# Side tasks queued ahead of the mask and exp of their step, in a two-layer graph kernel

## The chip, the core and the metric

The kernel runs on one core of a Trainium2 chip. The metric is the device time of one launch in microseconds (us). Before the change it was 3613.7 us, the median of three runs (3613.04 to 3614.69); the profiled execution took 3614.43 us, with a span of 3612.6 us from first to last instruction and a granted TensorE clock of 0.994.

## The reference

The first layer is a graph convolution over a 2048-node graph with two batch norms; the second is attention over the same graph, with 4 heads of 64, where only pairs with a nonzero entry in the adjacency take part. Each layer ends with a residual sum and a layer norm.

```python
# layer 0: A_hat @ features, two linear layers with batch norm
agg = jnp.einsum('nm,bmd->bnd', A_hat, features)
...
out = _batchnorm(out, g2, be2)
x = _layernorm(x + _L0_gnn_ref(...), axis=-1)
# layer 1: masked attention
qkv = h @ W
scores = jnp.einsum('bhid,bhjd->bhij', q, k) / np.sqrt(HEAD_DIM) + mask
attn = jax.nn.softmax(scores, axis=-1)
out = jnp.einsum('bhij,bhjd->bhid', attn, v)
x = _layernorm(x + _L1_gnn_ref(x, L1_gnn_W, adj), axis=-1)
```

x is 8 x 2048 x 256 in float32, so there are 8 batches, and everything is computed in float32.

## The kernel before

The change touches the second layer alone, which begins at about 1276 us and takes the other two thirds of the span. The attention is cut into 64 units: 8 batches, 2 pairs of heads, 4 chunks of 512 query columns. A unit has 16 steps, one for each tile of 128 keys. The loop variable `g` counts the steps over all units; `u` is the unit and `j` the step in it.

One step does this for its tile:

- `scores` (L842, TensorE): q times k, in 64x64 pieces for two heads, into a PSUM tile `st`, of which there are two.
- `mask_scores` (L854, VectorE): adds the mask to `st` and writes the SBUF tile `prob`, of which there are 13.
- `exps` (L860, ScalarE): exp of `prob` in place.
- `weigh` (L872, TensorE): `prob` times v, summed over the 16 steps in the PSUM tile `out_ps`.
- `add_up` (L882 to L893, GpSimd): sums `prob` tiles for the softmax's denominator, partly with adding transfers.

`scores`, `mask_scores` and `exps` run three steps ahead of `weigh` (`LEAD = 3`): in step `g` of the loop stand the scores, mask and exp of tile `g + 3` and the weighing of tile `g`.

Beside this there are side tasks: the projections of q, k and v of coming units, the normalization of the next batch's input, and the end of the unit before (its sums, the division by them, the residual, the layer norm, the output). Each has a due time, `at_step(u, j, f, ...)`: the whole part of `j` names the step, and the tasks of a step run in the order of `j`. A due time that is a whole number, such as 6, and one with a fraction, such as 6.1, were treated alike before. The tasks that the text speaks of:

- `finish_sums` (due 6): matmuls with ones (L909) sum `acc` over its partitions into a PSUM tile `pm`; ScalarE copies it out as `sm` (L917).
- `project` (before: due 0.1, 6.1, 10.1, for q, k, v): matmuls into `pm` (L777 for q and k, L791 for v); q and v are copied out by ScalarE (L782, L798), k by VectorE (L786).
- `norm` (half 0 due 6.2, half 1 due 0 of the next unit): four transposes into `pm` (L711), then on VectorE the residual sum (L719) and statistics (L660, L662). It runs in 28 units.
- `finish_turn_sums` (due 10): two transposes of `sm` (L923), a copy and a reciprocal on VectorE (L925, L930); `finish_turn` (10.2) transposes the unit's output (L936), and `finish` (10.3 and, before, 11) divides and adds on VectorE (L944).
- `emit` (due 4 and 5) and `apply` (due 7 and 8): each half is two normalizing activations on ScalarE (L672). `bn` (due 3.5 and 4.7): one each on ScalarE (L696).
- `turn` (due 13 and 13.2): four transposes for each half (L740) and a copy on ScalarE (L746). `emit_stats` (due 12.5 and 14): statistics on VectorE. `root` (due 3 or 15.5): four small operations on GpSimd.

All the `pm` tiles come from one PSUM pool with two buffers, taken in turn: a task that asks for one waits until the use before last has been read out. The engines TensorE, VectorE, ScalarE and GpSimd run their instructions in the order in which this loop emits them (`manual_schedule`), so the order of the Python calls is the order of each queue. Waits between engines are semaphores that the framework puts in.

Of the kernel before, what the change touches and what calls it, by code (L numbers as in the profile page):

```python
# [26 lines left out]
def tile_gcn_then_masked_attention(  # L27
# [169 lines left out]
    with tc.tile_pool(name="bt7", bufs=1, side="right") as bp7, tc.tile_pool(  # L197
# [20 lines left out]
        for n, t in enumerate(order):  # L218
# [7 lines left out]
            j, m = divmod(t, HT)  # L226
            k, q = divmod(m, TPC)
            here = slice(q * P, (q + 1) * P)
            for g in range(NT // 4):
# [4 lines left out]
                i, m0 = divmod(4 * g, HT)  # L234
# [574 lines left out]
    def attention():  # L809


        with tc.tile_pool(
# [8 lines left out]
            inp = Layer1Input(ip, ps_m, NCH + 4)  # L821
# [11 lines left out]
            def scores(g):  # L833
                u, j = divmod(g, NT)
                b, hp, c = units[u]
                qt, kt, _ = inp.qkv[b, hp]
                cols = slice(c * CH, (c + 1) * CH)
                st = ps_s.tile([P, 2, CH], F32, name="st")
                for h in range(2):
                    hs = slice(h * HD, (h + 1) * HD)  # L840
                    for r in range(2):
                        nc.tensor.matmul(  # L842
                            st[r * HD : (r + 1) * HD, h, :],
                            kt[hs, j * P + r * HD : j * P + (r + 1) * HD],
                            qt[hs, cols],
                            start=True, stop=True,
                        )
                return st

            def mask_scores(g, st):  # L850
                j, cols = g % NT, units[g // NT][2] * CH
                cols = slice(cols, cols + CH)
                p = probs[g] = ap_.tile([P, 2, CH], F32, name="prob", bufs=13)
                nc.vector.scalar_tensor_tensor(  # L854
                    p, mask[:, j, cols][:, None, :].to_broadcast([P, 2, CH]), MASKED, st,
                    op0=ALU.mult, op1=ALU.add,
                )

            def exps(g):
                nc.scalar.activation(probs[g], probs[g], AF.Exp)  # L860
# [34 lines left out]
            def finish_out(u):  # L895
                ots[u] = ap_.tile([P, CH], F32, name="ot")
                nc.scalar.copy(ots[u], outs[u][:, 0, :])
                nc.vector.tensor_add(ots[u], outs.pop(u)[:, 1, :], ots[u])  # L898
# [69 lines left out]
            side = {}  # L968

            def at_step(u, j, f, *args):  # L970
                tasks = side.setdefault((u, int(j)), [])
                tasks.append((j, f, args))
                tasks.sort(key=lambda task: task[0])

            per_b = HP * NCH
            for u in range(NU):
                b, hp, c = units[u]
                at_step(u + 1, 6, finish_sums, u)
                at_step(u + 1, 10, finish_turn_sums, u)
                at_step(u + 1, 10.2, finish_turn, u)  # L980
                at_step(u + 1, 10.3, finish, u, 0)
                at_step(u + 1, 11, finish, u, 1)
                if u == NU - 2:
                    for half in range(2):
                        at_step(u + 1, 11.3 + half, inp.emit_stats, b, c, half)
                        at_step(u + 1, 14 + half, inp.emit, b, c, half)
                    at_step(u + 1, 12.5, inp.root, b, c)
                elif u == NU - 1:
                    for half in range(2):
                        at_step(u + 1, 10.4 + half, inp.emit_stats, b, c, half)  # L990
                        at_step(u + 1, 10.5 + half, inp.root_half, b, c, half)
                        at_step(u + 1, 12 + half, inp.emit_half, b, c, half)
                    at_step(u + 1, 14, count_sums)
                elif hp == HP - 1:
                    for half in range(2):
                        at_step(u + 1, 12.5 + 1.5 * half, inp.emit_stats, b, c, half)
                        at_step(u + 2, 4 + half, inp.emit, b, c, half)
                    at_step(u + 1, 15.5, inp.root, b, c)

            PROJECT = (0.1, 6.1, 10.1)

            def project_at(u, b, hp, c):
                for w in range(3):
                    at_step(u, PROJECT[w], inp.project, b, hp, c, w)

            for b in range(B):
                u0 = b * per_b
                if b:  # L1010
                    project_at(u0, b, 0, NCH - 1)
                for c in range(NCH):
                    project_at(u0 + 1 + c, b, 1, c)
                    if b + 1 == B:
                        continue
                    u = u0 + 3 + c
                    at_step(u, 1, inp.load_y, b + 1, c)
                    at_step(u, 1, inp.load_x, b + 1, c)
                    for o in range(NO):
                        at_step(u, 3.5 + 1.2 * o, inp.bn, b + 1, c, o)  # L1020
                    at_step(u, 6.2, inp.norm, b + 1, c, 0)
                    at_step(u + 1, 0, inp.norm, b + 1, c, 1)
                    at_step(u + 1, 3, inp.root, b + 1, c)
                    for half in range(2):
                        at_step(u + 1, 7 + half, inp.apply, b + 1, c, half)
                        at_step(u + 1, 13 + 0.2 * half, inp.turn, b + 1, c, half)
                    if c < NCH - 1:
                        project_at(u + 2, b + 1, 0, c)
# [3 lines left out]
                for half in range(2):  # L1032
                    at_step(0, j, inp.turn, 0, c, half)
            for half in range(2):
                at_step(0, 1, inp.apply, 0, 3, half)
            for j, c, w in (
                (1.1, 1, 2), (2.1, 2, 1), (5.1, 2, 2), (6.1, 3, 1), (8.1, 1, 0), (10.1, 3, 2)
            ):
# [4 lines left out]
            with tc.manual_schedule(engines=IN_ORDER):  # L1043
                for c in range(NCH):
                    inp.yt[0, c] = y0[c]
                    inp.x1[0, c] = ip.tile([P, TPC, D], F32, name="x1", bufs=NCH + 4)
                    for o in range(NO):
                        inp.bn(0, c, o)

                def ready(c):  # L1050
                    pm = ps_s.tile([P, TPC, D], F32, name="st")
                    for half in range(2):
                        pmh = pm[:, half * IT : (half + 1) * IT, :]
                        inp.turn_y(0, c, half, pmh)
                        inp.add_y(0, c, half, pmh, x0[c])
                    inp.root(0, c)

                def halves(f, c):
                    for half in range(2):
                        f(0, c, half)  # L1060

                for c in range(NCH - 1):
                    ready(c)
                halves(inp.apply, 0)
                halves(inp.turn, 0)
                halves(inp.apply, 1)
                inp.project(0, 0, 0, 1, k_on_act=True)
                inp.project(0, 0, 0, 0)
                ready(NCH - 1)
                right.close()  # L1070
                ap_ = inp.y_pool = late.enter_context(
                    tc.tile_pool(name="attn", bufs=2, side="right", reuse_waits="tile")
                )
                inp.project(0, 0, 0, 2)
                halves(inp.turn, 1)
                for g in range(LEAD):
                    mask_scores(g, scores(g))
                    exps(g)
                    if g == 1:
                        inp.project(0, 0, 1, 1)  # L1080
                        halves(inp.apply, 2)
                for g in range(NU * NT):
                    u, j = divmod(g, NT)
                    ahead = g + LEAD < NU * NT
                    if ahead:
                        st = scores(g + LEAD)
                    if j == NT - 1:
                        weigh(g)
                        finish_out(u)
                    if ahead:  # L1090
                        mask_scores(g + LEAD, st)
                        exps(g + LEAD)
                    for _, f, args in side.get((u, j), ()):
                        f(*args)
                    if j < NT - 1:
                        weigh(g)
                    add_up(g)
                for u in (NU, NU + 1):
                    for j in range(NT):
                        for _, f, args in side.get((u, j), ()):  # L1100
                            f(*args)

    def attention_with_maxima():

        with tc.tile_pool(name="full", bufs=2) as ap_, tc.tile_pool(
# [9 lines left out]
            for b in range(B):  # L1115
# [55 lines left out]
                for c in range(NCH):  # L1171
# [3 lines left out]
                    for half in range(2):  # L1175
                        inp.emit(b, c, half)

    attention()


# [46 lines left out]
```

## Time and profile before

| Engine | busy us | share of the span |
| --- | --- | --- |
| TensorE (matmul) | 3553.4 | 98% |
| GpSimd | 2265.8 | 63% |
| VectorE | 1994.5 | 55% |
| ScalarE | 1635.0 | 45% |

| Durations, second layer | mean us of one | number |
| --- | --- | --- |
| mask L854 (VectorE) | 1.218 | 1024 |
| exp L860 (ScalarE) | 1.056 | 1024 |
| sum of prob tiles L893 (GpSimd) | 2.60 | 319 |
| copy of sm L917 (ScalarE) | 0.353 | 64 |
| normalizing activation L672 (ScalarE) | 0.586 | 256 |

The first table reads: TensorE is almost never without a matmul, and every other engine is idle for over a third of the span. The second says how long a side task holds an engine in comparison with the mask or exp of a step; in the timeline a step of scores and weighing without side tasks takes 1.72 us (scores start at 1550.57, 1552.29, 1554.01 us and so on).

### The profile page before, as it was taken

The numbers are of one execution on the slowest core, as the hardware profiler recorded it, in microseconds if no ns is written. First come the engines' busy times: TensorE is split into PE (matmuls) and PEld (weight loads), VectorE is DVE, ScalarE is ACT, GpSimd is POOL, SyncE is SP. The second block draws the span as 40 slices with busy tenths as digits, with TensorE's granted clock in tenths as the row PEclk, the third lists the DMA queues.
The fourth block names the chain that finished last, engine by engine and source line by source line (L and its number), as shares of the span: only waits on it lengthen the run. The fifth ranks groups of instructions, "written<-read, shape, count | busy, mean of one in ns | idle before, by whom it ended". The sixth has DMA issues, their size and how long they took to land.

```text
span 3612.6 us, 55141 instructions
## 1 busy us (share of the span) xinstructions
PE 3553.4 (98%) x22503; PEld 1469.7 (41%) x22503; DVE 1994.5 (55%) x2929; ACT 1635.0 (45%) x2036; POOL 2265.8 (63%) x1530
## 2 busy tenths in 40 slices
PE   8999999999999899999999999999999999999997
PEld 5444444444444443433333333333343334343332
DVE  6212141221146656676766776676666677667666
ACT  5101100110135455655565565565566566556555
POOL 3543263434247647776777677777777777777777
PEclk9999999999999999999999999999999999999999
DMA  9122232231247345666565666556566556555655
GB/s 340 65 72 88 81 134 82 76 96 32 82 187 267 143 91 103 127 126 123 112 141 119 119 131 132 108 123 141 112 123 133 117 112 148 112 117 113 122 109 115
DMA packets 197142, 440.14 MB, mean 122 GB/s; under 512 B 14080, under 2 KB 121104, under 8 KB 186384
## 3 DMA queue, kind: packets, MB, share of 16 engines
q0 software_dynamic: 64656, 239.37, 35.0%
q1 hardware_dynamic: 132048, 196.11, 15.8%
q8 instruction: 178, 2.92, 0.3%
q10 hardware_dynamic: 176, 1.06, 0.1%
q14 instruction: 84, 0.69, 0.1%
HBM read 126.62 MB, written 75.51 MB: 56 GB/s over the span
## 4 chain that ended last, share of the span: by engine, by line
PE 95%; ACT 2%; DVE 2%; POOL 1%; DMA 0%; issue 0%; DVEq 0%; POOLq 0%; ACTq 0%; SPq 0%
PE out_ps L872 25%; PE st L842 24%; PE pa L333 21%; PE ph L366 5%; PE pm L777 5%; PE pa L543 5%; PE pm L791 3%; DVE prob L854 1%; PE pm L711 1%; ACT prob L860 1%; PE pm L740 1%; PE pm L936 1%; PE pm L923 1%; PE ps L233 1%; PE pm L909 1%; PE ph L588 1%
## 5 line engine op out<-in xcount | busy, mean ns | idle before, releaser
L854 DVE SCALAR_TENSOR_TENSOR prob<-mask,st 128x1024 f32<-128x1024 uint8 x1024 | 1242.0, 1218 | 486.1 <-PE st L842 412.2
L860 ACT ACTIVATE prob<-prob 128x1024 f32<-128x1024 f32 x1024 | 1081.0, 1056 | 930.0 <-DVE prob L854 838.5
L872 PE MATMUL out_ps<-prob,v 64*64 64x512 f32 x8192 | 1074.2, 595 | 2.7 <-DVE ot L898 1.7
L842 PE MATMUL st<-qt,kt 64*64 64x512 f32 x8192 | 1062.8, 589 | 0.1
L893 POOL TENSOR_TENSOR acc<-acc,prob 128x1024 f32<-128x1024 f32 x319 | 829.7, 2601 | 8.0 <-DMA prob<-prob 2.6
L333 PE MATMUL pa<-t,x 128*128 128x512 f32 x1792 | 773.4, 594 | 2.7 <-ACT x L309 2.7
L882 POOL DMA_DIRECT2D prob<-prob x447 | 403.7, 928 | 582.5 <-PE out_ps L872 503.3
L842 PEld LDWEIGHTS st<-qt,kt 64*64 64x64 f32 x8192 | 312.6, 133 | 566.7 <-issue 538.0
L333 PEld LDWEIGHTS pa<-t,x 128*128 128x128 f32 x1792 | 341.4, 191 | 432.7 <-issue 428.7
L872 PEld LDWEIGHTS out_ps<-prob,v 64*64 64x64 f32 x8192 | 290.7, 133 | 541.6 <-issue 445.7
L414 POOL TENSOR_TENSOR ag<-ag,dbc 128x512 f32<-128x512 f32 x16 | 20.2, 1261 | 486.3 <-DVE ag L413 454.8
L884 POOL TENSOR_TENSOR acc<-acc,prob 128x1024 f32<-128x1024 f32 x126 | 298.1, 2366 | 7.5
L370 ACT ACTIVATE h<-ph,b1s 128x512 f32<-128x512 f32 x112 | 76.9, 687 | 404.4 <-PE ph L366 404.4
L777 PE MATMUL pm<-x1t,wq 128*128 128x512 f32 x512 | 253.1, 617 | 0.7 <-ACT x1t L746 0.7
L394 ACT COPY ag<-pa 128x512 f32<-128x512 f32 x16 | 9.4, 585 | 422.9 <-PE pa L333 409.8
L366 PE MATMUL ph<-ag,w1s 128*128 128x512 f32 x448 | 193.4, 592 | 0.0
L891 POOL TENSOR_TENSOR acc<-prob 128x1024 f32<-128x1024 f32 x64 | 171.2, 2675 | 1.7 <-DMA prob<-prob 1.7
L944 DVE SCALAR_TENSOR_TENSOR x<-pm,ri,x 128x64 f32<-128x64 f32 x512 | 109.6, 277 | 62.4 <-PE pm L936 61.7
L672 ACT ACTIVATE x<-x,ln_nm,ln_rs 128x256 f32<-128x256 f32 x256 | 137.6, 586 | 10.5 <-POOL ln_nm L668 10.5
L777 PEld LDWEIGHTS pm<-x1t,wq 128*128 128x128 f32 x512 | 87.8, 191 | 119.8 <-issue 113.0
L371 DVE BATCH_NORM_STATS2 st<-h 128x6 f32<-128x512 f32 x112 | 76.9, 692 | 99.1 <-ACT h L370 99.1
L366 PEld LDWEIGHTS ph<-ag,w1s 128*128 128x128 f32 x448 | 85.1, 190 | 107.1 <-issue 106.9
(139 smaller groups left out, 2609.0 us busy)
## 6 DMA issues: line engine op xcount, KB each, us to landing
prob<-prob POOLq DMA_DIRECT2D x447, 512.0 KB, 4.9
x<-in_x_dram SPq DMA_DIRECT2D x92, 512.0 KB, 5.4
h_d<-h SPq DMA_DIRECT2D x28, 1024.0 KB, 3.9
t<-h_d SPq DMA_DIRECT2D x28, 1024.0 KB, 8.2
a<-in_adj_dram SPq DMA_DIRECT2D x16, 1024.0 KB, 5.0
y_d<-ag SPq DMA_DIRECT2D x32, 512.0 KB, 2.6
out_dram<-x SPq DMA_DIRECT2D x31, 512.0 KB, 4.9
yt<-y_d SPq DMA_DIRECT2D x28, 512.0 KB, 3.3
```

The lines of the kernel that those rows point to most:

```text
L333: nc.tensor.matmul(pa, s.t[:, m, :], t[:, m, :], start=(m == 0), stop=(m == HT - 1))
L366: nc.tensor.matmul(ph, w1s[:, d, f * P : (f + 1) * P], ag[:, d, :], start=(d == 0), stop=(d == ND - 1),)
L543: nc.tensor.matmul(py, w[:, f, :], t[:, f, :], start=(f == 0), stop=(f == 1))
L777: nc.tensor.matmul(pm, wq[:, d, wcols], xt[:, d, cols], start=(d == 0), stop=(d == ND - 1))
L842: nc.tensor.matmul(st[r * HD : (r + 1) * HD, h, :], kt[hs, j * P + r * HD : j * P + (r + 1) * HD], qt[hs, cols], start=True, stop=True,)
L854: nc.vector.scalar_tensor_tensor(p, mask[:, j, cols][:, None, :].to_broadcast([P, 2, CH]), MASKED, st, op0=ALU.mult, op1=ALU.add,)
L860: nc.scalar.activation(probs[g], probs[g], AF.Exp)
L872: nc.tensor.matmul(outs[u][hs, r, :], inp.qkv[b, hp][2][rs, j, hs], probs[g][rs, h, :], start=(j == 0), stop=(j == NT - 1),)
L882: nc.gpsimd.dma_start(probs[g - 1], probs[g], accum_op=ALU.add)
L884: nc.gpsimd.tensor_add(accs[u], accs[u], probs[g])
L891: nc.gpsimd.tensor_add(accs[v], probs[g - 7], probs[g - 5])
L893: nc.gpsimd.tensor_add(accs[v], accs[v], probs[g - 5])
```

## The change

Side tasks whose due time is exactly a whole step are now called before the mask and exp of that step, and those with a fraction after them, as before. The call of `scores` stays ahead of all of them and that of `weigh` behind. Four due times that were whole, or had to stay behind a task that was moved, get another fraction, so that these tasks keep their places: `finish` half 1, `norm` half 1, the projection of q, and the `apply` of the first unit.

The purpose is that work which others wait for, such as the copy of `sm` out of PSUM, doesn't stand in its engine's queue behind a mask or exp that nobody needs for three steps.

```diff
-                at_step(u + 1, 11, finish, u, 1)
+                at_step(u + 1, 11.1, finish, u, 1)
...
-            PROJECT = (0.1, 6.1, 10.1)
+            PROJECT = (0.2, 6.1, 10.1)
...
-                    at_step(u + 1, 0, inp.norm, b + 1, c, 1)
+                    at_step(u + 1, 0.1, inp.norm, b + 1, c, 1)
...
-                at_step(0, 1, inp.apply, 0, 3, half)
+                at_step(0, 1.05, inp.apply, 0, 3, half)
...
                     if j == NT - 1:
                         weigh(g)
                         finish_out(u)
+
+                    tasks = side.get((u, j), ())
+                    for i, f, args in tasks:
+                        if i == j:
+                            f(*args)
                     if ahead:
                         mask_scores(g + LEAD, st)
                         exps(g + LEAD)
-                    for _, f, args in side.get((u, j), ()):
-                        f(*args)
+                    for i, f, args in tasks:
+                        if i > j:
+                            f(*args)
                     if j < NT - 1:
                         weigh(g)
                     add_up(g)
```

## Prediction

> **What bounds the kernel now.** I read the page's first part, then its chain of waits, then the list of who TensorE waited for, then the timeline around the longest entry.
>
> ```profile
> PE 3553.4 (98%) x22503; PEld 1469.7 (41%) x22503; DVE 1994.5 (55%) x2929; ACT 1635.0 (45%) x2036; POOL 2265.8 (63%) x1530
> PE 95%; ACT 2%; DVE 2%; POOL 1%; DMA 0%; issue 0%; DVEq 0%; POOLq 0%; ACTq 0%; SPq 0%
> ```
>
> TensorE sets the time: 95% of the chain that ended last is its own work. What a reordering of other engines can win is at most its idle time, 3612.6 - 3553.4 = 59 us, or 1.6%. The waits of TensorE (us in total, times, longest) say where that idle time is:
>
> ```profile
> PE pm L711 <- ACT sm L917: 15.7, 28, 1.4
> PE st L711 <- ACT ag L696: 6.1, 2, 5.9
> PE pc L243 <- DMA a<-in_adj_dram: 5.8, 1, 5.8
> PE pm L909 <- POOL acc L893: 3.6, 1, 3.6
> PE out_ps L872 <- ACT prob L860: 1.0, 1, 1.0
> ```
>
> The first line is the only one that recurs through the attention: 28 times the transposes of `norm` wait for the copy of `sm`. The second and third lie before the attention, the last two after the last scores. At step 6 `finish_sums` takes one `pm` buffer, `project` the other, and `norm` wants the first again, which is free once ScalarE has copied `sm`. The timeline shows what that copy stands behind (start us, duration us, engine, line):
>
> ```profile
> 1410.11 1.06 ACT L860 ACTIVATE prob<-prob 128x1024 f32<-128x1024 f32 x1
> 1410.39 0.64 PE L909 MATMUL pm<-acc,ones 128*32 128x256 f32 x8
> 1410.96 1.98 PE L777 MATMUL pm<-x1t,wq 128*128 128x512 f32 x4
> 1411.85 1.06 ACT L860 ACTIVATE prob<-prob 128x1024 f32<-128x1024 f32 x1 [0.68 <-DVE prob L854]
> 1412.81 0.35 ACT L917 COPY sm<-pm 128x256 f32<-128x256 f32 x1
> 1413.22 0.66 PE L711 MATMUL pm<-ident,yt 128*128 128x128 f32 x4 [0.28 <-ACT sm L917]
> 1413.81 1.09 PE L872 MATMUL out_ps<-prob,v 64*64 64x512 f32 x8
> ```
>
> The sums are ready at 1410.39 + 0.64 = 1411.03, and ScalarE is idle from 1411.17. But the step's exp is ahead in its queue, waiting for the mask until 1411.85; so the copy ends only at 1413.16. The second form of the wait is longer:
>
> ```profile
> 2103.47 1.98 PE L777 MATMUL pm<-x1t,wq 128*128 128x512 f32 x4
> 2103.58 1.04 ACT L860 ACTIVATE prob<-prob 128x1024 f32<-128x1024 f32 x1
> 2104.53 1.08 ACT L672 ACTIVATE x<-x,ln_nm,ln_rs 128x256 f32<-128x256 f32 x2
> 2105.51 1.04 ACT L860 ACTIVATE prob<-prob 128x1024 f32<-128x1024 f32 x1
> 2106.45 0.35 ACT L917 COPY sm<-pm 128x256 f32<-128x256 f32 x1
> 2106.86 0.66 PE L711 MATMUL pm<-ident,yt 128*128 128x128 f32 x4 [1.41 <-ACT sm L917]
> ```
>
> Here the unit also has `emit` and `bn` in steps 3 to 5, ScalarE runs without a pause since 2099.19, and the exp is late itself. One unit per batch boundary is of this kind: two pairs of heads end while the next batch is normalized. With n long and 28 - n short waits, 1.41 n + 0.28 (28 - n) = 15.7 gives n = 7, as seven batch boundaries should.
>
> **What the Trainium skill says.** "TensorE: Matmul & The Clock Gate", section "Architectural detail: the array is 16× 32×32, not 1× 128×128", states that ScalarE and VectorE queues are strictly first in, first out, while TensorE may pull weight loads ahead. The trace agrees: ScalarE idles 0.68 us before the exp with a ready copy behind it. "Perfetto Trace Analysis", section "Tensor Engine Instruction (MATMUL, LD_WEIGHTS)", states that the end of a matmul in the profile is a model. The trace agrees: L777's bar of 1.98 us is overlapped by the next matmul, 1.92 us after its start where nothing is waited for. I therefore price waits by start to start, not by the idle figures.
>
> **The change part by part.** TensorE, GpSimd and the DMA queue keep the order of their instructions; only ScalarE and VectorE are reordered. No operation is added or removed.
>
> 1. *Copy of `sm` (63 of 64 units).* The three windows from the scores of step 6 to the next weighing, which the timeline gave, are
>
> ```profile
> 1409.42:1413.81 4.39, 4.11 (x29) 1.41 (x21) 2.53 (x3) 3.07 (x5) 0.00 (x0) 1.00 0.89 166
> 1559.16:1562.61 3.45, 3.45 (x25) 0.99 (x17) 1.83 (x2) 3.45 (x7) 1.55 (x2) 1.00 0.73 134
> 2101.93:2107.44 5.51, 4.11 (x28) 1.41 (x20) 2.52 (x3) 4.87 (x9) 1.57 (x2) 1.00 0.83 155
> ```
>
> (first number: length). The second has no `norm`. Four transposes with no wait take 0.53 us from start to start (L936 at 1571.70, L872 at 1572.23). So the short wait really costs 4.39 - 3.45 - 0.53 = 0.41 us, the long one 5.51 - 3.98 = 1.53. After the change the copy of the short case starts at 1411.17, when the exp before it ends, and is out by 1411.6; `norm` may start at 1410.96 + 1.92 = 1412.88. The wait goes: 21 x 0.41 = 8.6 us. In the long case ScalarE is saturated, and its queue up to the copy is shorter by one exp only, which takes 2106.45 - 2105.51 = 0.94 us from start to start. The transposes move from 2106.86 to 2105.92, where 2103.47 + 1.92 = 2105.39 would be free: 0.53 us of wait stay. Gain 7 x 0.94 = 6.6 us. **Sum 15.2 us.** In the other units nobody waits for the copy, and nothing is won.
>
> 2. *What the copy delays.* The exp behind it, by 0.35 us at most, and the semaphore wait on L909, which is done 0.14 us before ScalarE is free. The exp's tile is weighed three steps, over 5 us, later. Cost 0.
>
> 3. *`finish_turn_sums` (63 times).* VectorE now holds the mask of step 10 until the transposes L923 are done: 1420.84 + 0.44 = 1421.28, then 0.17 + 0.20 for copy and reciprocal, so the mask starts near 1421.7 instead of 1420.97 and ends near 1422.9. Behind it: `finish` half 0, which waits for TensorE until 1423.54 anyway; the exp and the copy of v, 0.7 us later; and the scores of step 12, which need this `st` buffer only at 1426.05. `finish_turn` gets its `pm` sooner than before. Cost 0, with 3 us of slack.
>
> 4. *`emit` and `apply` (58 units' worth, two halves of 1.07 us on ScalarE) ahead of an exp.* Their inputs come from `root` steps earlier (done 2101.39, used from 2111.75), so they don't wait; an exp comes up to 1.07 us later. In the saturated unit the last late exp ends near 2106.9 and is weighed after 2111. Cost 0, hidden behind scores and weighing.
>
> 5. *`turn` half 0 and `emit_stats` half 1.* The copy L746 (0.58) fits into ScalarE's pause before the exp at 2085.73, the statistics (0.75 + 0.30) into VectorE's 1.15 us before the mask at 2086.84. Cost 0. `root` and the loads stand on queues without mask or exp.
>
> 3613.7 - 15.2 = **3598.5 us**, 0.42% less.
>
> **The rivals.**
>
> - *The long waits go too.* If the applied activations start in earlier pauses, ScalarE is not saturated at the copy: 21 x 0.41 + 7 x 1.53 = 19.3 us, 3594.4. Against it: no pause is left from 2099.19 on.
> - *Only the short waits go.* If `emit`'s move hands the 0.94 us back in the seven long units: 3613.7 - 8.6 = 3605.1. For it: ScalarE is full there. Against: the work ahead of the copy gets less whatever the order.
> - *The wait moves on.* The time saved at `norm` is lost at the weighing behind it, to GpSimd (busy for 1591 of 2160 us in the attention) or to an exp: 3612, no difference. Against: weighings show no wait on either in the attention.
> - *Slower.* If the mask of step 10, 0.7 us later in 63 units, reached the path, 63 x 0.7 = 44 us would be lost against 15 won: 3643 at worst. The scores of step 12 do gain a wait on VectorE that others covered before. Against: the 3 us of slack in point 3.
>
> **How the numbers follow.** Forecast 0.68, all waits gone 0.12, short ones only 0.12, moved on 0.05, slower 0.03. The first three are faster by over 0.2% (7.2 us): 0.92; same 0.05, slower 0.03. The range reaches from just below 3594.4 up to 3604, which takes in the forecast with a few us of small new waits, and leaves out most of the last three.
>
> **What would show it.** The list of TensorE's waits should have L711 on `sm` 7 times with some 0.5 us each, or not at all, instead of 28; ScalarE should show the copy ahead of the exp in step 6; step 6 with `norm` should take 3.98 us; the 63 masks of step 10 should stand after the reciprocal, with scores starting every 1.72 us as before. Any new line of TensorE waiting for L854, L860 or L672 above 3 us in total makes the prediction wrong.

## The result, and the profile after

The changed kernel takes 3597.44 us (median of four runs, 3594.16 to 3597.93) against 3614.11 us: the ratio is 0.9952, with a 95% interval of 0.9935 to 0.997. It is faster by 16.7 us, where 15.2 us were forecast.

The two profiled executions differ by more, 3612.6 against 3592.4 us of span. Part of that is not the change: the first scores of the attention start at 1275.3 us before and at 1272.2 us after, and ahead of them nothing was changed. From the first to the last weight load of the scores (L842) the attention takes 3585.5 - 1275.3 = 2310.2 us before and 3565.5 - 1272.2 = 2293.3 us after, **16.9 us less**. The granted clock over the attention was 1.00 in both, and in every kernel below, so this length compares like with like. I use it beside the timed medians.

The engines' busy time on the page after (us, share of the span, instructions):

```profile
PE 3545.7 (99%) x22503; PEld 1470.5 (41%) x22503; DVE 1989.2 (55%) x2929; ACT 1637.4 (46%) x2036; POOL 2265.2 (63%) x1530
```

The instructions are as many as before on every engine; TensorE's idle time fell from 59 to 3592.4 - 3545.7 = 47 us. (Its busy sum fell as well, by 7.7 us; as the ends of matmuls are modelled, I don't read a gain from that.) The list of what TensorE waited for in the kernel after (us in total, times, longest):

```profile
PE st L711 <- ACT ag L696: 6.1, 2, 5.9
PE pc L243 <- DMA a<-in_adj_dram: 5.7, 1, 5.7
...
PE pm L909 <- POOL acc L893: 3.6, 1, 3.6
...
PE pm L711 <- ACT sm L917: 2.6, 7, 0.4
PE out_ps L872 <- DVE ot L898: 2.6, 3, 1.0
```

The wait that headed the list has shrunk from 28 times and 15.7 us to 7 times and 2.6 us; the waits outside the attention are the same to 0.2 us. The last line is new among the larger ones: it was 1.7 us before, and is taken up below. No wait of a matmul for the mask (L854), the exp (L860) or the activations of `emit` and `apply` (L672) is new or has grown. The timeline of a step 6 with a short wait, in the kernel after:

```profile
1407.00 1.06 ACT L860 ACTIVATE prob<-prob 128x1024 f32<-128x1024 f32 x1
1407.27 0.64 PE L909 MATMUL pm<-acc,ones 128*32 128x256 f32 x8
1407.84 1.98 PE L777 MATMUL pm<-x1t,wq 128*128 128x512 f32 x4
1407.98 0.37 ACT L917 COPY sm<-pm 128x256 f32<-128x256 f32 x1
1408.74 1.06 ACT L860 ACTIVATE prob<-prob 128x1024 f32<-128x1024 f32 x1 [0.38 <-DVE prob L854]
1409.66 0.60 PE L711 MATMUL pm<-ident,yt 128*128 128x128 f32 x4
1410.19 1.09 PE L872 MATMUL out_ps<-prob,v 64*64 64x512 f32 x8
```

The copy of `sm` now stands in the pause in which ScalarE waited for the mask, and the exp behind it isn't late: it still waits 0.38 us for the mask. The transposes follow the projection without a gap. A step 6 of the other kind:

```profile
2093.80 1.98 PE L777 MATMUL pm<-x1t,wq 128*128 128x512 f32 x4
2093.83 1.07 ACT L672 ACTIVATE x<-x,ln_nm,ln_rs 128x256 f32<-128x256 f32 x2
2094.81 1.04 ACT L860 ACTIVATE prob<-prob 128x1024 f32<-128x1024 f32 x1
...
2095.76 0.35 ACT L917 COPY sm<-pm 128x256 f32<-128x256 f32 x1
...
2096.01 1.05 ACT L860 ACTIVATE prob<-prob 128x1024 f32<-128x1024 f32 x1
2096.16 0.65 PE L711 MATMUL pm<-ident,yt 128*128 128x128 f32 x4 [0.37 <-ACT sm L917]
```

`emit` (L672) is now ahead of the exp, but it is still ahead of `sm` too, and ScalarE is full; one exp fewer stands before the copy, and 0.37 us of wait are left by the profile. The lengths of these two steps, from the scores to the next weighing (first number), in windows of the kernel after:

```profile
1406.31:1410.19 3.88, 3.88 (x28) 1.49 (x20) 2.15 (x3) 3.10 (x5) 0.00 (x0) 1.00 0.99 187
2092.27:2096.74 4.47, 4.10 (x28) 1.41 (x20) 2.52 (x3) 4.47 (x7) 1.57 (x2) 1.00 0.79 147
```

They were 4.39 and 5.51 us. So the change wins 21 x 0.51 + 7 x 1.04 = 18.0 us there, and gives about 1 us back elsewhere.

### The profile page after: what moved, and what is told of

Its sections match the earlier page's. It is cut to its first block, busy times and chain, and to the rows that moved or that the text cites. A ratio compares the mean times of both kernels' runs of the same rounds, so it can differ in the third digit from the quotient of the medians.

```text
span 3592.4 us, 55051 instructions
## 1 busy us (share of the span) xinstructions
PE 3545.7 (99%) x22503; PEld 1470.5 (41%) x22503; DVE 1989.2 (55%) x2929; ACT 1637.4 (46%) x2036; POOL 2265.2 (63%) x1530
## 5 line engine op out<-in xcount | busy, mean ns | idle before, releaser
L860 ACT ACTIVATE prob<-prob 128x1024 f32<-128x1024 f32 x1024 | 1081.2, 1056 | 913.1 <-DVE prob L854 836.8
L854 DVE SCALAR_TENSOR_TENSOR prob<-mask,st 128x1024 f32<-128x1024 uint8 x1024 | 1239.1, 1215 | 434.4 <-PE st L842 358.4
L842 PE MATMUL st<-qt,kt 64*64 64x512 f32 x8192 | 1062.8, 589 | 0.1
L842 PEld LDWEIGHTS st<-qt,kt 64*64 64x64 f32 x8192 | 312.5, 133 | 566.7 <-issue 526.4
L672 ACT ACTIVATE x<-x,ln_nm,ln_rs 128x256 f32<-128x256 f32 x256 | 137.5, 586 | 10.5 <-POOL ln_nm L668 10.5
```

What stands on the lines that cost most here:

```text
L672: nc.scalar.activation(self.t[:, i, :], self.t[:, i, :], AF.Identity, bias=self.nm[:, i : i + 1], scale=self.rs[:, i : i + 1],)
L842: nc.tensor.matmul(st[r * HD : (r + 1) * HD, h, :], kt[hs, j * P + r * HD : j * P + (r + 1) * HD], qt[hs, cols], start=True, stop=True,)
L854: nc.vector.scalar_tensor_tensor(p, mask[:, j, cols][:, None, :].to_broadcast([P, 2, CH]), MASKED, st, op0=ALU.mult, op1=ALU.add,)
```

## The experiments

Theory: the whole gain is that the copy of `sm` left the queue behind the exp; the other moved tasks cost nothing and bring nothing. Rivals: other moved tasks bring a part; putting side tasks first is good in itself; the gain comes from masks and exps that come at other times.

| Kernel | us, median | ratio to before (95%) | attention, us | waits for `sm` |
| --- | --- | --- | --- | --- |
| before | 3613.8 to 3614.1 | 1 | 2310.2 | 28, 15.7 us |
| after | 3597.44 | 0.9952 (0.9935 to 0.997) | 2293.3 | 7, 2.6 us |
| sums alone ahead | 3596.52 | 0.9951 (0.9937 to 0.9964) | 2293.1 | 7, 3.2 us |
| all but the sums ahead | 3614.32 | 1.0 (0.9992 to 1.0009) | 2310.4 | 28, 15.1 us |
| all tasks ahead | 3607.8 | 0.9984 (0.9978 to 0.9991) | 2305.1 | none |
| after, `emit` later | 3592.69 | 0.994 (0.9926 to 0.9953) | 2289.2 | none |
| before, `emit` later | 3605.98 | 0.9978 (0.9969 to 0.9987) | 2302.3 | 28, 7.8 us |
| before, `norm` later | 3601.15 | 0.9965 (0.9953 to 0.9977) | 2297.1 | none |
| after, all of step 10 ahead | 3598.0 | 0.9952 (0.9938 to 0.9965) | 2293.3 | 7, 2.6 us |
| after, `emit` later, statistics back | 3592.0 | 0.9939 (0.9925 to 0.9952) | 2288.3 | none |

### The sums alone, and all but the sums

```diff
-                        if i == j:
+                        if f is finish_sums:
...
-                        if i > j:
+                        if f is not finish_sums:
```

> Only the sums of step 6 (finish_sums) are called ahead of the mask and exp; all other tasks stay behind, as before. Theory (the copy of sm is the whole gain): as fast as the changed kernel, 3596 to 3598 us against 3614 before; the transposes of norm wait for sm 7 times, 2.6 us in all, instead of 28 times and 15.7 us. Rival (the other moved tasks bring a part): less than the change, such as 3602 to 3608 us.

```diff
-                        if i == j:
+                        if i == j and f is not finish_sums:
...
-                        if i > j:
+                        if i > j or f is finish_sums:
```

> The changed kernel with finish_sums alone put back behind the mask and exp; all the other whole-step tasks stay ahead. Theory: the gain is gone, 3613 to 3616 us, and norm waits for sm 28 times again, near 15.7 us. Rival (the other moved tasks bring a part): 3602 to 3608 us.

What TensorE waited for in the kernel with the sums alone ahead, and then with all but the sums:

```profile
PE pm L711 <- ACT sm L917: 3.2, 7, 0.5
...
PE out_ps L872 <- DVE ot L898: 1.7, 3, 0.6
```

```profile
PE pm L711 <- ACT sm L917: 15.1, 28, 1.3
...
PE out_ps L872 <- DVE ot L898: 2.6, 3, 1.0
```

One task has the whole gain: alone ahead, it gives 2310.2 - 2293.1 = 17.1 us of attention; without it, 0.2 us are lost. The theory holds, and the rival that other tasks bring a part of any size falls.

The other moved tasks do two small things that nearly cancel. In the seven units with a long wait they shorten the wait for `sm` by 0.6 us in all (15.1 us where they are ahead against 15.7; and 2.6 against 3.2, where the sums alone were expected to reach 2.6). In one such unit of each kernel, the time on ScalarE from the last exp that waited long for its mask to the copy of `sm` is 7.26 us before, 7.18 with all but the sums, 6.32 with the sums alone and 6.23 after. The timelines show where these 0.08 to 0.09 us lie: in step 4 the exp started 0.77 us after `bn` began, as its mask was not done; with `emit` ahead of the exp, `emit` starts there after 0.70 us. On the other side, the wait for the sum of the output (L898) is 2.6 us where the other tasks are ahead and 1.7 us where they aren't.

### All tasks ahead

```diff
-                        if i == j:
+                        if i >= j:
...
-                        if i > j:
+                        if i < j:
```

> All side tasks of a step ahead of its mask and exp, those with fractions too. Theory (only what waits for nothing late may go ahead): the mask of step 6 stands behind the copy of k, the sum and the statistics of norm, ends about 0.85 us after the scores of step 8 could start, in 28 units: 24 us lost against the change, about 3621 us (3613 to 3628), and TensorE shows a new wait of the scores for the mask. Rival (ahead is better or free, as the slack of three steps covers it): 3597 us or less.

The time is 10 us above the change's. TensorE's waits and the timeline of step 6 to 8 in this kernel:

```profile
PE st L842 <- DVE prob L854: 8.9, 28, 0.3
```

```profile
1412.54 0.69 DVE L786 COPY kt<-pm 128x512 f32<-128x512 f32 x1 [2.95 <-PE pm L777]
...
1413.15 0.68 DVE L719 TENSOR_TENSOR x<-pm,x 128x512 f32<-128x512 f32 x1
1413.78 1.04 PE L842 MATMUL st<-qt,kt 64*64 64x512 f32 x8
1413.87 0.75 DVE L660 BATCH_NORM_STATS2 ln_st<-x 128x6 f32<-128x256 f32 x2
...
1414.75 3.62 DVE L854 SCALAR_TENSOR_TENSOR prob<-mask,st 128x1024 f32<-128x1024 uint8 x3
...
1415.99 1.09 PE L842 MATMUL st<-qt,kt 64*64 64x512 f32 x8 [0.32 <-DVE prob L854]
...
1416.90 1.04 PE L872 MATMUL out_ps<-prob,v 64*64 64x512 f32 x8
```

The new wait is there, 28 times: VectorE stands idle for 2.95 us until the projection of k is done, the scores of step 8 start 2.21 us after those of step 7 instead of 1.72, and the weighing behind them 0.91 us later instead of 0.86. So "ahead is better" falls. The size was half of what I expected, and the time below the range that I gave. I had added up bars on VectorE, 0.69 + 0.69 + 0.76 + 0.30 and pauses, to 2.50 us between the copy of k and the mask; from start to start it is 1414.75 - 1412.54 = 2.21 us. 28 x 0.54 = 15.1 us are lost and 7 x 0.59 = 4.1 us won back where the wait for `sm` is gone altogether, 11.0 in all; the attention shows 2305.1 - 2293.3 = 11.8 us, so 0.8 us of it are not assigned.

### `emit` at another place

```diff
-                    at_step(u + 2, 4 + half, inp.emit, b, c, half)
+                    at_step(u + 2, 9 + 2 * half, inp.emit, b, c, half)
```

> The changed kernel with the two halves of emit at steps 9 and 11 in place of 4 and 5, so that ScalarE is not full before step 6 in the seven units where a batch ends while the next is normalized. Theory: the wait of 7 times 0.37 us that is left goes, and step 6 of these units takes 3.88 us as in the others in place of 4.47: 7 x 0.59 = 4 us less, about 3593.4 us. Rival (emit at its new place makes another wait, for the copy of v or of the output): the wait on sm goes, but the time stays at 3597 or more.

Then the same in the kernel before, with 9.4 in place of 9:

> The kernel before, with the two halves of emit due at 9.4 and 11.4 in place of 4 and 5 (still behind mask and exp). Theory (the seven long waits are long only because emit fills ScalarE in steps 4 and 5): they become short ones, norm waits 28 times for 0.28 us, 7.8 us in all, and the time falls by 7 x (5.51 - 4.39) = 7.8 us to about 3606 us. Rival (the exps are late there for another reason, such as bn or the mask): 3612 us or more, and waits of over 1 us stay.

The timeline of the changed kernel with `emit` later, in a unit that had the long wait:

```profile
2094.24 0.64 PE L909 MATMUL pm<-acc,ones 128*32 128x256 f32 x8
...
2094.81 1.98 PE L777 MATMUL pm<-x1t,wq 128*128 128x512 f32 x4
2094.95 0.37 ACT L917 COPY sm<-pm 128x256 f32<-128x256 f32 x1
...
2096.63 0.60 PE L711 MATMUL pm<-ident,yt 128*128 128x128 f32 x4
```

The copy starts 0.71 us after L909 does, as in the other units, and the transposes wait for nothing. The attention is 2293.3 - 2289.2 = 4.1 us shorter than after the change alone, as expected. In the kernel before, TensorE's waits with `emit` later were

```profile
PE pm L711 <- ACT sm L917: 7.8, 28, 0.3
```

28 short waits, and 2310.2 - 2302.3 = 7.9 us less, as expected (7.8). Both together show the cause of the long waits: `emit` beside `bn` on ScalarE in steps 4 and 5. The 2.6 us that the change left were its doing.

### The wait taken away by another route

```diff
-                    at_step(u, 6.2, inp.norm, b + 1, c, 0)
+                    at_step(u, 7.2, inp.norm, b + 1, c, 0)
```

> The kernel before, with half 0 of norm due at 7.2 in place of 6.2, so that its pm buffer has been read out long before; the order of sm, mask and exp is as before. Theory (the wait for the pm buffer is all that the change takes away): no wait on sm; 21 x 0.51 + 7 x 1.63 = 22.1 us won, less some 28 x 0.16 = 4.5 us, since the transposes are now a block of their own between 64x64 matmuls: about 3596.5 us. Rival (the gain comes from exps and masks that come at other times): about 3614 us, as before.

With ScalarE's order as before, and only the sum and statistics of `norm` one step later on VectorE, 2310.2 - 2297.1 = 13.1 us of attention go. So the gain is in the wait for the buffer, and doesn't need the exp behind the copy. It is less than the 17.6 us expected, and the timeline of this kernel shows why:

```profile
1407.73 1.98 PE L777 MATMUL pm<-x1t,wq 128*128 128x512 f32 x4
...
1409.64 1.09 PE L872 MATMUL out_ps<-prob,v 64*64 64x512 f32 x8
...
1410.55 1.04 PE L842 MATMUL st<-qt,kt 64*64 64x512 f32 x8
1411.52 0.66 PE L711 MATMUL pm<-ident,yt 128*128 128x128 f32 x4
...
1412.11 1.09 PE L872 MATMUL out_ps<-prob,v 64*64 64x512 f32 x8
...
1413.02 1.04 PE L842 MATMUL st<-qt,kt 64*64 64x512 f32 x8
```

As a block of their own the transposes make step 7 last 1413.02 - 1410.55 = 2.47 us, 0.75 more than 1.72, and the projection before them is followed after 1.91 us. Behind the projection, in the kernel after, the two take 1.82 + 0.53 = 2.35 us. That is 1.91 + 0.75 - 2.35 = 0.31 us in each of 28 units, 8.7 us, and not the 0.16 that I took. 22.1 - 8.7 = 13.4 us; 13.1 were measured.

### How late may a mask be, and what is given back

```diff
-                        if i == j:
+                        if i == j or j == 10:
...
-                        if i > j:
+                        if i > j and j != 10:
```

> The changed kernel with all the tasks of step 10 ahead of its mask and exp, so with half 0 of finish too. Theory (a late mask costs nothing until the scores two steps later want its st buffer): the mask of step 10 ends near 1422.0 us where the change's unit has its scores of step 12 at 1422.44; no loss, within 2 us of the change. Rival (the slack is smaller than read, or the semaphores take more than 0.4 us): each of some 60 units loses 0.2 to 0.5 us, 12 to 30 us in all, with the scores waiting for the mask.

The attention is 2293.3 us, as after the change. The timeline of this kernel at steps 10 to 12:

```profile
1420.61 0.44 PE L923 MATMUL pm<-ident,sm 128*128 128x128 f32 x2
...
1423.31 0.86 DVE L944 SCALAR_TENSOR_TENSOR x<-pm,ri,x 128x64 f32<-128x64 f32 x4 [1.81 <-PE pm L936]
1424.09 2.42 DVE L854 SCALAR_TENSOR_TENSOR prob<-mask,st 128x1024 f32<-128x1024 uint8 x2
...
1425.83 1.04 PE L842 MATMUL st<-qt,kt 64*64 64x512 f32 x8
```

The first of the two masks starts 3.48 us after the transposes L923, where before the change it was 0.13 us (1420.84 and 1420.97), and ends near 1424.09 + 1.22 = 1425.31. The scores that need its buffer start at 1425.83 without a wait. Step 10 has this room because two groups of transposes and the projection of v stand in it: its scores started at 1419.64 and the next ones at 1424.11, 4.47 us later instead of 1.72. A mask can be over 3 us late in step 10 at no cost; in step 6 of the kernel with all tasks ahead, a mask that reaches into the scores two steps later costs TensorE at once.

Last, the statistics of step 14 go back behind the mask, together with the later `emit`:

```diff
-                        at_step(u + 1, 12.5 + 1.5 * half, inp.emit_stats, b, c, half)
+                        at_step(u + 1, 12.5 + 1.6 * half, inp.emit_stats, b, c, half)
```

> The changed kernel with emit at steps 9 and 11, and with half 1 of emit_stats due at 14.1, so behind the mask and exp of step 14. Theory: in the last units, which have no turn in step 13, the statistics ahead of the mask made the copy of the output late; back behind, the three waits of the first weighing of a unit for the output's sum fall from 2.6 to 1.7 us in all, 0.9 us less than with emit alone later: about 3592 us, not to be told from it by time. Rival: the waits stay at 2.6 us.

The end of a unit among the last, before the change and after it (timeline of each):

```profile
3532.12 0.59 ACT L897 COPY ot<-out_ps 128x512 f32<-128x512 f32 x1 [0.26 <-PE out_ps L872]
...
3533.49 1.09 PE L872 MATMUL out_ps<-prob,v 64*64 64x512 f32 x8 [0.57 <-DVE ot L898]
```

```profile
3508.68 0.75 DVE L660 BATCH_NORM_STATS2 ln_st<-x 128x6 f32<-128x256 f32 x2
...
3509.56 1.19 DVE L854 SCALAR_TENSOR_TENSOR prob<-mask,st 128x1024 f32<-128x1024 uint8 x1
...
3510.78 1.06 ACT L860 ACTIVATE prob<-prob 128x1024 f32<-128x1024 f32 x1 [0.93 <-DVE prob L854]
3511.75 0.57 ACT L897 COPY ot<-out_ps 128x512 f32<-128x512 f32 x1
...
3513.09 1.09 PE L872 MATMUL out_ps<-prob,v 64*64 64x512 f32 x8 [1.00 <-DVE ot L898]
```

After the change the copy of the output no longer waits for TensorE but for the exp ahead of it, which is late because its mask (L854) stood behind the statistics (L660). With the statistics back, TensorE's waits have

```profile
PE out_ps L872 <- DVE ot L898: 1.7, 3, 0.6
```

and the attention is 2288.3 us, 0.9 us shorter than with `emit` later alone: the expected size, which the timed medians (3592.0 and 3592.69) can't tell. By the length of the attention this is the fastest version; its time is 0.61% below the kernel before (0.48% to 0.75% by the interval).

## Why the prediction was right

The direction, the mechanism and the place were right, and the time was 1.1 us from the forecast. Point by point:

1. *Copy of `sm`.* Right, with two terms that were mis-sized: 18.0 us in place of 15.2. The short waits cost 0.51 us and not 0.41: I let the transposes start 1.92 us after the projection, which is the distance to a 64x64 weighing; between the projection and the transposes it is 1409.66 - 1407.84 = 1.82 us. The long ones won 5.51 - 4.47 = 1.04 us and not 0.94. The one exp fewer brought what was forecast (7.26 - 6.32 = 0.94 us with the sums alone ahead); the other 0.09 us are `emit`'s, which starts earlier in step 4. I had read that ScalarE has no pause from 2099.19 us on, since its bars follow without a gap; but the exp at 2100.93 waited for its mask, which ended only at 2099.67 + 1.22 = 2100.89. That 7 waits would stay was right: 0.37 us each by the profile where some 0.5 were expected, and 4.47 - 3.88 = 0.59 us from start to start.
2. *The exp behind the copy.* Right: no cost, shown by the sums alone giving the whole gain.
3. *`finish_turn_sums`.* Right: the mask of step 10 follows the reciprocal in the kernel after,

```profile
1417.22 0.44 PE L923 MATMUL pm<-ident,sm 128*128 128x128 f32 x2
...
1417.91 0.20 DVE L930 RECIPROCAL ri<-sums_all 128x8 f32<-128x8 f32 x1
1418.03 1.17 DVE L854 SCALAR_TENSOR_TENSOR prob<-mask,st 128x1024 f32<-128x1024 uint8 x1
```

0.81 us after the transposes start (0.86 was worked out), and it costs nothing, as a delay four times as long doesn't either.

4. *`emit` and `apply`.* Right that they cost nothing: no wait of theirs reached TensorE. That they bring nothing was wrong by the 0.09 us in seven units.
5. *`turn` and `emit_stats`.* Wrong by 0.9 us. The pause of 1.15 us before the mask of step 14 was read in a unit with `turn` in step 13, which makes that step longer. The last units have no `turn`, so there the statistics delay the mask, the exp and the copy of the output, and the first weighing of the next unit waits 0.43 us more, twice.

18.0 - 0.9 = 17.1 us against the measured 16.9. (The 18.0 multiplies one unit of each kind, rounded; over all 28 units of the two traces, step 6 became 17.7 us shorter, and the first weighings of two units cost 0.9.) The two errors have opposite signs, and the nearness of the forecast owes a little to that. Of the rivals, "moved on" and "slower" didn't happen; what speaks against both is the pair of the first two experiments. "Only the short waits go" fell as well, as the long steps became 1.04 us shorter. "The long waits go too" had a cause that exists, the activations in an earlier pause, but it was worth 0.09 us a unit and left all 7 waits.

## What to carry to other kernels

Where an engine works through its queue in order, look for a short instruction that the bounding engine waits for and that stands behind a long one which itself waits: it can be moved into that pause for nothing, and here only that one needed to move. A task whose own input comes late must stay behind, and how much later a mask may come was set here by the next user of the PSUM tile that it reads, not by the consumer three steps on. Bars that follow without a gap don't prove that nothing is waited for. Price such moves from start to start of the same pair of neighbours, and read the slack in every kind of unit, the last ones too.

## What the runs showed of the hardware

The time that TensorE took from one group to the next depended on what followed: after the 128x128 projection, transposes of the same tile size started after 1.82 us and 64x64 matmuls after 1.91 to 1.92 us, and a group of four transposes put between two 64x64 groups cost 0.75 us in place of 0.53 us behind another 128x128 group. On VectorE the bars of neighbours overlap: four groups of operations with bars of 2.42 us in all (0.69, 0.68, 0.75, 0.30) were followed by a mask 2.21 us after the start of the first.
